# A graph attention whose keys are sorted within and across partitions, with bf16 one-hot sums and the payload in three parts

## The chip, the cores and the metric

The kernel runs on one core of a Trainium2 chip. The metric is the device time of one execution in microseconds (us), taken as the median of several runs. The profile comes from one further execution; its instructions are counted from the first one's start.

## The reference, cut to what matters

Four layers follow each other on 6250 nodes of 256 features, each with a layer norm before it and its result added to x. The change lies in the second: an attention over 131072 random edges (both ends drawn from 0 to 8191, so that many fall outside the nodes), whose result chooses two of four experts for each node.

```python
h = (x_flat @ W_gat).reshape(M, HEADS, NUM_EXPERTS)          # 4 x 4
a_src = (h * att_src).sum(-1); a_dst = (h * att_dst).sum(-1)
e = leaky_relu(a_src[src] + a_dst[dst], negative_slope=0.2)
ee = exp(e - segment_max(e, dst)[dst])
denom = segment_sum(ee, dst, num_segments=M)
msg = h[src] * (ee / (denom[dst] + 1e-16))[:, :, None]
agg = segment_sum(msg, dst, num_segments=M).reshape(M, 16) + b_gat
scores = layernorm(agg).reshape(M, HEADS, NUM_EXPERTS).mean(1)
topk_s, topk_i = top_k(scores, 2); w = softmax(topk_s)
for ei in range(4):                                          # 256 -> 512 -> 256
    out += gate(ei) * (gelu(x @ W1[ei] + b1[ei]) @ W2[ei] + b2[ei])
```

The first layer is a graph layer over 106250 edges with 256 attributes each (sorted by destination), the third a graph layer over the same edges with one weight each, the fourth a small mixture of experts. Source indices beyond the last node count as the last node; edges with a destination outside the nodes are left out.

## The kernel before, in words

The nodes lie in T = 49 blocks of 128. Three stages follow each other.

**Edge stage** (loop over `q` in the function's middle, to about 1555 us). The first layer's edges come in 147 groups (`groups1`, three a block of nodes). Each group is turned on DVE (`turn`, L1487 on), multiplied on PE (`hidden`), joined with gathered rows on DVE (`join`, L1505), rectified on ACT and summed on PE (`add_up`, L1512). [...]the order of the queues is the order of the program text here (`Ordered.pin`). Beside it runs other work, one generator step at a time (`steps`, L1611): `sort` is the sorting of the attention's keys, one step a group, and `slow` the preparation of the edges' windows.

Sorting: each partition holds C2 = 1024 of the attention's edges as integer keys (destination in the high bits, source in the low 13), made by `make_keys`. `sort_steps` (L1284) is a bitonic sort of the 1024 keys within each partition: 55 passes, each of a max and a min (L1299, L1300), the first 45 in two runs. `sorted_edges` (L1307) then takes the keys apart into the source (`src2`), the block of the destination (`high`) and its place in the block (`low`), writes `low` turned to DRAM (`low_dram`), and compares all blocks with limits (L1329 to L1338), so that an edge outside its limits starts `general_path` at the end.

**Attention stage** (loop `for k in range(NA + 5)`, L2208, 1555 to about 2830 us). A tile is one column of the sorted keys: one edge from each of the 128 partitions. A row `g` is eight tiles; there are NA = 80 rows. Since each partition is sorted by itself, a row's edges fall into a band of up to NK = 12 blocks (`near_blocks`, L932; 9.9 blocks in the mean). Row `g` goes through these steps, in iterations g, g+2, g+3, g+4 and g+5 of the loop:

- `fetch` (L1793): eight gathers on POOL of the source nodes' 24 values, five buffers.
- `score` (L1798): rb, the turned `low` broadcast from DRAM, is compared with the partition number (L1806, DVE), and PE multiplies the resulting one-hot rows with `part`, the destination scores of the band in three bf16 parts, into pa (L1810, three matmuls a tile). A (L1818) is the one-hot choice of the block.
- `weigh` (L1824): za = pa times A, reduced over blocks, plus the source's score, leaky, exponential (ACT).
- `spread_out` (L1838), in halves of four tiles: the payload (16 values and 4 denominators times the exponential, L1845, in PSUM as px) is spread over the band, pp = payload times A (L1852), 20 columns a block; B (L1861) is the one-hot place in the block, fp32.
- `add_up` (L1866): for each tile one fp32 matmul of B with pp, 20 columns a block, summed over the eight tiles in po (L1873); then acc += po (L1879, DVE).

Between these stand "slots" (`slot`, L2187): each issues one step of the second layer's experts (`experts1`; four fp32 matmuls ph or py of 256 columns, L1115), in the first 62 iterations five a row and then four, 396 steps in all, and steps of the node work. `count_last` (L1882) counts the edges whose source is the last node, by columns 544 to 848, eight at a time, two groups an iteration. When the sums of a range of blocks are complete (`complete`), `gates` makes the choice of experts and `node_values` the next layer's table `hp_dram`. ys of the experts are loaded back by `load_outputs` into eight buffers.

**Last stage** (from about 2875 us): gathers of `hp_dram` (831 on POOL), the third layer's sums and the fourth layer.

Of the kernel before, what the change touches and what calls it, by code (L numbers as in the profile page):

```python
# [16 lines left out]
P = 128  # L17
# [10 lines left out]
class Ordered:  # L28
# [6 lines left out]
    def pin(self):  # L35
# [16 lines left out]
        self.at = self.traced[-1]  # L52

# [815 lines left out]
def kernel(ctx: ExitStack, tc: tile.TileContext, a: dict, out: bass.AP):  # L869
# [49 lines left out]


    KA, KB, KT, KM, NK = 640, 544, 848, 596.0, 12
# [3 lines left out]
    assert C2 % 8 == 0 and KA % P == 0 and P % G == 0 and N <= 8192 - P and T >= NK  # L925
# [5 lines left out]

    def near_blocks(g):  # L932

        k = g * G + G / 2
        mid = k * (N / KM) / P
        spread_of = (C2 * (k / C2) * (1 - k / C2)) ** 0.5 * (N / KM) / P
        n = min(NK, int(-(-2 * (4.2 * spread_of + 0.9) // 1)))
        b0 = min(max(round(mid - n / 2), 0), T - 2)
        return b0, min(max(round(mid - n / 2) + n, b0 + 2), T) - b0
# [4 lines left out]
    with ExitStack() as fast:  # L944
# [12 lines left out]
        lane16 = const.tile([P, P], BF16, name="lane16")  # L957
        with tc.tile_pool(name="numbers", bufs=1) as numbers:
# [6 lines left out]
            V.tensor_copy(lane16, jn)  # L965
# [281 lines left out]
        src2 = gat.tile([P, KA], I32, name="src2")  # L1247
        low = gat.tile([P, KT], BF16, name="low")
        high = gat.tile([P, KT], BF16, name="high")
        good3 = gat.tile([P, 2, 2], F32, name="good3")  # L1250

        def make_keys(ix, k):
# [4 lines left out]
            for i in range(2):  # L1257
# [22 lines left out]
                raw[1], raw[1], 13, 0x10000000, op0=OP.logical_shift_left, op1=OP.bitwise_or  # L1280
# [3 lines left out]
        def sort_steps():  # L1284


            here, there = key, order
            size = 2
            while size <= C2:
                step = size // 2  # L1290
                while step:
# [13 lines left out]
            assert here is order  # L1305

        def sorted_edges(pst, wk):  # L1307

            k = order.bitcast(I32)[:, 0:KT]
            V.tensor_scalar(src2, k[:, 0:KA], 8191, None, op0=OP.bitwise_and)  # L1310
            some = key[:, 0:KT]
            for v, s in ((high, 20), (low, 13)):
                vi = some.bitcast(I32)
                V.tensor_scalar(
                    vi, k, s, 127, op0=OP.logical_shift_right, op1=OP.bitwise_and
                )
                V.tensor_copy(some, vi)
                V.tensor_scalar(some, some, -1.0, 127.0, op0=OP.mult, op1=OP.add)
                V.tensor_copy(v, some)
            for c in range(KA // P):  # L1320
                pt = pst.tile([P, 4, P], F32, name="pt")
                TE.transpose(pt[:, 0, :], some[:, c * P : (c + 1) * P], ident)
                lt = wk.tile([P, P], BF16, name="lt")
                SC.activation(lt, pt[:, 0, :], AF.Copy)
                SC.dma_start(low_dram[c * P : (c + 1) * P, :], lt)
            V.tensor_add(good2[:, 1:2], good3[:, 0, 0:1], good3[:, 1, 0:1])
            V.tensor_add(good2[:, 3:4], good3[:, 0, 1:2], good3[:, 1, 1:2])

            lim = key[:, 0:KA]  # L1329
            for g in range(KA // G):  # L1330
                V.memset(lim[:, g * G : (g + 1) * G], float(near_blocks(g)[0]))
            hit = order[:, 0:KA]
            V.tensor_tensor(hit, high[:, 0:KA], lim, op=OP.is_ge)
            for g in range(KA // G):
                V.memset(lim[:, g * G : (g + 1) * G], sum(near_blocks(g)) - 0.5)
            V.tensor_tensor(lim, lim, high[:, 0:KA], op=OP.is_ge)
            V.tensor_mul(hit, hit, lim)
            V.tensor_reduce(good2[:, 0:1], hit, axis=AX.X, op=OP.add)  # L1338
# [5 lines left out]
        with ExitStack() as layer:  # L1344
# [113 lines left out]
            HS = D + 8  # L1458
            with (
# [144 lines left out]
                def sorting():  # L1604

                    yield from sort_steps()
                    sorted_edges(psm, wk)
# [13 lines left out]
                for q in range(NQ1 + 2):  # L1621
# [15 lines left out]
                    steps()  # L1637
# [19 lines left out]
        acc = sums.tile([P, T, HV], F32, name="acc")  # L1657
# [101 lines left out]
        with (  # L1759
# [4 lines left out]
            tc.tile_pool(name="pa3", bufs=2, space=PSUM) as psa,  # L1764
            tc.tile_pool(name="po3", bufs=1, space=PSUM) as pso,
            tc.tile_pool(name="px3", bufs=1, space=PSUM) as psx,
# [9 lines left out]
            px = psx.tile([P, P + 2 * G * HV], F32, name="px")  # L1776
            lanes = px[:, 0:P]
            V.tensor_copy(lanes, lane)
# [3 lines left out]
            NA = KA // G  # L1782
# [55 lines left out]
            def spread_out(g, half):  # L1838
# [18 lines left out]
                if half == 1:  # L1857
                    near.pop(g)
# [789 lines left out]
```

## Time and profile before

| | |
|---|---|
| median of 3 runs | 4254.52 us (4244.25 to 4271.54) |
| profiled execution | 4184.73 us |
| its span, first to last instruction | 4182.9 us |
| mean granted TensorE clock | 0.857 |
| busy: PE, PEld, DVE, ACT, POOL | 3303.4, 2578.7, 2138.8, 1127.3, 2249.3 us |
| attention: matmuls po (L1873) | 1280 records, 261.1 us busy |
| attention: matmuls pa (L1810, bf16) | 1920, 76.8 us |
| experts: ph and py (L1115) | 1600 and 1568 records, 417.1 and 408.4 us |
| gathers in the three stages | 882, 640 and 831 on POOL |

PE is TensorE's matmuls, PEld its weight loads, DVE VectorE, ACT ScalarE, POOL GpSimd, SP the engine that issues most transfers. A group's row gives line, engine, operation, output and inputs, shape, count, then busy us and mean ns, then the idle time of the engine just before the group and what ended it ("issue": nothing that the profile shows; "remote": an event that it can't place). An fp32 matmul has two records. Records overlap in the pipeline, so that their mean is longer than their distance, and busy times of groups can overlap too.

### The profile page before, as it was taken

The numbers are of one execution on the slowest core, as the hardware profiler recorded it, in microseconds if no ns is written. First come the engines' busy times: TensorE is split into PE (matmuls) and PEld (weight loads), VectorE is DVE, ScalarE is ACT, GpSimd is POOL, SyncE is SP. The second block draws the span as 40 slices with busy tenths as digits, with TensorE's granted clock in tenths as the row PEclk, the third lists the DMA queues.
The fourth block names the chain that finished last, engine by engine and source line by source line (L and its number), as shares of the span: only waits on it lengthen the run. The fifth ranks groups of instructions, "written<-read, shape, count | busy, mean of one in ns | idle before, by whom it ended". The sixth has DMA issues, their size and how long they took to land.

```text
span 4182.9 us, 57093 instructions
## 1 busy us (share of the span) xinstructions
PE 3303.4 (79%) x18509; PEld 2578.7 (62%) x18509; DVE 2138.8 (51%) x5571; ACT 1127.3 (27%) x2014; POOL 2249.3 (54%) x2364
## 2 busy tenths in 40 slices
PE   6888888898898885888898998786256866767788
PEld 5566666666576664677787777674245544555566
DVE  6566566665554444656455657555223333333344
ACT  4122222222222222333434344452001211111123
POOL 0656556566565634455454545534666666666651
PEclk8899999999899997999999999896557677767778
DMA  5677777777676742323333334333111111111210
GB/s 174 158 176 167 163 168 168 162 169 163 154 176 164 168 109 53 82 66 89 88 81 101 97 85 111 72 77 95 44 47 49 51 50 49 51 49 51 53 50 20
DMA packets 699200, 428.56 MB, mean 102 GB/s; under 512 B 531305, under 2 KB 640348, under 8 KB 698893
## 3 DMA queue, kind: packets, MB, share of 16 engines
q0 software_dynamic: 89408, 178.08, 18.4%
q1 hardware_dynamic: 366236, 187.21, 16.9%
q10 hardware_dynamic: 243248, 59.52, 7.2%
q8 instruction: 150, 2.46, 0.3%
q14 instruction: 158, 1.29, 0.1%
HBM read 382.05 MB, written 42.49 MB: 101 GB/s over the span
## 4 chain that ended last, share of the span: by engine, by line
PE 50%; another core or an unknown queue 18%; DVE 7%; issue 6%; ACT 3%; DMA 1%; POOL 0%; SPq 0%; ACTq 0%; DVEq 0%
PE ph L1115 22%; PE py L1115 10%; PE pe L2513 5%; PE pt L1115 4%; PE po L1873 4%; PE pe L1531 3%; PE pa L1810 1%; DVE eq L2492 1%; PE pt L1109 1%; DMA rb<-low_dram 1%; ACT hh L1709 1%; PE pe L2508 1%; ACT L1709 0%; DVE x_all L2054 0%
## 5 line engine op out<-in xcount | busy, mean ns | idle before, releaser
L1128 POOL DMA_INDIRECT h<-y_dram,src x882 | 846.6, 960 | 666.5 <-issue 508.4
L1128 POOL DMA_INDIRECT hg<-hp_dram,src x831 | 785.7, 946 | 457.8 <-issue 229.1
L1128 POOL DMA_INDIRECT sg<-gat_dram,src x640 | 612.0, 956 | 623.0 <-DVE px L1845 339.0
L1115 PE MATMUL ph<-w1b,et 128*128 128x256 f32 x3528 | 863.3, 397 | 35.9 <-issue 25.7
L1115 PEld LDWEIGHTS ph<-w1b,et 128*128 128x128 f32 x3528 | 677.5, 197 | 205.3 <-issue 115.9
L2513 PE MATMUL pe<-eq,hg 128*128 128x96 f32 (+15 forms) x2036 | 372.6, 331 | 158.3 <-issue 100.6
L2513 PEld LDWEIGHTS pe<-eq,hg 128*128 128x128 f32 x2036 | 359.0, 250 | 224.9 <-issue 157.8
L1508 DVE TENSOR_TENSOR h<-ph,h 128x1536 f32<-128x1536 f32 x147 | 258.2, 1757 | 428.8 <-remote 149.4
L1115 PE MATMUL py<-w,hh 128*128 128x256 f32 x1568 | 408.4, 400 | 64.2 <-ACT hh L1709 33.7
L1115 PE MATMUL ph<-b_all,w 128*128 128x256 f32 (+1 forms) x1600 | 417.1, 400 | 11.3 <-issue 9.8
L2492 DVE TENSOR_SCALAR eq<-px,dst,ew 128x96 f32<-128x96 f32 x831 | 262.3, 372 | 319.3 <-remote 137.4
L1509 ACT ACTIVATE h<-h 128x1536 f32<-128x1536 f32 x147 | 218.2, 1485 | 725.4 <-DMA ea<-in_edge_attr_dram 293.2
L1115 PEld LDWEIGHTS py<-w,hh 128*128 128x128 f32 x1568 | 300.3, 199 | 118.1 <-ACT hh L1709 41.7
L1115 PEld LDWEIGHTS ph<-b_all,w 128*128 128x128 f32 x1600 | 307.8, 202 | 55.4 <-issue 16.6
L1531 PE MATMUL pe<-h,eq 128*32 128x257 f32 x3168 | 257.2, 412 | 41.2 <-issue 40.9
L1873 PE MATMUL po<-pp,B 128*128 128x240 f32 (+10 forms) x1280 | 261.1, 344 | 17.2 <-DVE acc L1879 7.1
L1709 ACT ACTIVATE hh<-ph,b 128x256 f32<-128x256 f32 (+1 forms) x400 | 165.7, 466 | 392.0 <-remote 151.0
L1490 DVE STREAM_TRANSPOSE et<-ea 128x1536 f32<-128x1536 f32 x147 | 260.5, 1773 | 13.1 <-issue 9.5
L1873 PEld LDWEIGHTS po<-pp,B 128*128 128x128 f32 x1280 | 220.4, 194 | 32.0 <-issue 8.4
L1531 PEld LDWEIGHTS pe<-h,eq 128*32 128x32 f32 x3168 | 106.1, 115 | 148.0 <-issue 100.9
L1115 PE MATMUL py<-ew,g 65*128 65x256 f32 x392 | 136.5, 474 | 68.2 <-DVE x_all L2468 58.2
L1852 DVE TENSOR_TENSOR pp<-px,A 128x960 f32<-128x960 f32 (+10 forms) x160 | 156.3, 977 | 39.9 <-remote 27.5
(339 smaller groups left out, 3808.8 us busy)
## 6 DMA issues: line engine op xcount, KB each, us to landing
ea<-in_edge_attr_dram ACTq DMA_DIRECT2D x588, 96.0 KB
ea<-in_edge_attr_dram SPq DMA_DIRECT2D x588, 96.0 KB
y<-y SPq DMA_DIRECT2D x196, 128.0 KB
w<-in_L_ffn_W_dram SPq DMA_DIRECT2D x48, 512.0 KB
y<-ys SPq DMA_DIRECT2D x96, 256.0 KB
rb<-low_dram SPq DMA_DIRECT2D x80, 256.0 KB
h<-y_dram,src POOLq DMA_INDIRECT x882
hg<-hp_dram,src POOLq DMA_INDIRECT x831
```

The lines of the kernel that those rows point to most:

```text
L1109: TE.transpose(pt[:, c, :], src[:, c * P : (c + 1) * P], ident)
L1115: TE.matmul(dst, lhs(c), rhs(c), start=c == 0, stop=c == n - 1)
L1128: GP.indirect_dma_start(out=dst, out_offset=None, in_=table[0:NP, :], in_offset=IndirectOffsetOnAxis(ap=idx, axis=0),)
L1490: V.transpose(et[q].rearrange("p c m k -> p m c k"), ahead.pop(q).rearrange("p i m (c k) -> p (i m) c k", c=2),)
L1508: V.tensor_add(h, ph.pop(q), h)
L1509: SC.activation(h, h, AF.Relu)
L1531: TE.matmul(sums[w][b * Q : (b + 1) * Q, :], eq[k][:, j, at], h[:, i * NT + j, 0:WS], start=g == 0 and j == NT - 1, stop=g == last_of[b] a ...
L1709: SC.activation(hidden[u][:, f, :n, :], ph[:, f - f0, :n, :], AF.Gelu, bias=b1[:, e, f : f + 1],)
L1852: V.tensor_tensor(pps[g, half][:, :, 0:n, :], pay[:, js, :].unsqueeze(2).to_broadcast([P, HG, n, HV]), near[g][:, js, 0:n].unsqueeze(3).to ...
L1873: TE.matmul(po.rearrange("p b v -> p (b v)"), B[:, j, :], pp[:, j, 0:n, :].rearrange("p b v -> p (b v)"), start=half == 0 and j == 0, stop ...
L2492: V.tensor_scalar(equals[k][:, j, :], lanes[:, 0:NW], dst_of[:, t : t + 1], ew[:, t : t + 1], op0=OP.is_equal, op1=OP.mult,)
L2513: TE.matmul(sums[b][:, lo - t0 * P : hi - t0 * P], hg[:, j, :], eq[:, j, lo - n0 : hi - n0], start=False, stop=after >= (t0 + n) * P,)
```

## The change

**Sorting across partitions.** `sort_steps` gets an argument `least` and is run twice. The first run sorts within partitions and stops the last merge at steps of 8, so that each group of eight columns holds the right eight keys, in no order. `turn_keys` turns the keys on PE (eight transposes, two ACT copies), so that partition r holds row r's 1024 keys from all partitions; the second run sorts these, stopping the last merge at steps of 128; a second turning brings them back. A tile then holds 128 keys that follow each other in a whole row. Each step is still a max and a min and a `yield`; `sort` is now advanced twice in odd groups. `sorted_edges` yields between its parts, and its comparison with limits goes.

**Fewer blocks a tile.** `sorted_tiles` works out on the host, for each tile, which blocks its edges can fall into. For these sizes there are NA = 84 rows, 73 of them with eight tiles, 612 tiles together; a tile covers 1 to 7 blocks, 2116 in all, and a row a union of up to 14. `block` holds for each edge its block less the first of its tile; its starting values are written by 379 POOL memsets when the kernel starts.

**Sums.** For each tile E is a one-hot [128, blocks x 128] in bf16: one DVE `tensor_scalar` compares the numbers `nodes16` with the edge's number (`bits`), both as bf16 patterns. The payload is split into three bf16 parts (`weight`), which with a column of ones make 61 columns (`pays`, two buffers). PE multiplies E, a block at a time, with the payload; a row's sums lie in two PSUM banks of up to eight blocks each, the first with two buffers, the second with one. acc has 61 columns a block; `gates` adds the three parts, and the ones count the edges for the check at the end.

```diff
-        def sort_steps():
+        def sort_steps(here, there, least):
...
-                while step:
+                while step >= (least if size == C2 else 1):
...
+        def turn_keys(pst, here, there):
+            for k in range(0, G, 4):
+                pt = pst.tile([P, 4, P], F32, name="pt")
+                for i in range(4):
+                    TE.transpose(pt[:, i, :], here[:, :, k + i], ident)
+                SC.activation(there[:, k : k + 4, :], pt, AF.Copy)
+                yield
+        def sort_all(pst):
+            yield from sort_steps(key, order, G)
+            yield from turn_keys(
+                pst, key.rearrange("p (r k) -> p r k", k=G),
+                order.rearrange("p (k r) -> p k r", k=G),
+            )
+            yield from sort_steps(order, key, P)
+            yield from turn_keys(
+                pst, order.rearrange("p (k r) -> p r k", k=G),
+                key.rearrange("p (r k) -> p k r", k=G),
+            )
...
-                    steps()
+                    steps(*([sort] if q % 2 else []))
...
-                got[g] = wk.tile([P, G, GW], F32, name="sg", bufs=5)
+                got[g] = wk.tile([P, G, GW], F32, name="sg", bufs=4)
...
+            def weight(g, step):
+                m = len(tiles2[g])
+                parts = [pays[g % 2][:, 0:m, i * HV : (i + 1) * HV] for i in range(3)]
+                if step == 0:
+                    pay[g] = wk.tile([P, G, HV], F32, name="pay", bufs=1)[:, 0:m, :]
...
+                    SC.activation(parts[0], pay[g], AF.Copy)
+                elif step == 1:
+                    V.tensor_sub(pay[g], pay[g], parts[0])
+                    SC.activation(parts[1], pay[g], AF.Copy)
+                else:
+                    V.tensor_sub(parts[2], pay.pop(g), parts[1])
+            def spread_out(g, j):
...
+                n = tiles2[g][j][1]
+                Es[g, j] = wk.tile([P, NM, P], BF16, name="E", bufs=EB)
+                V.tensor_scalar(
+                    Es[g, j][:, 0:n, :].rearrange("p b k -> p (b k)"), nodes16[:, 0 : n * P],
+                    bits.bitcast(F32)[:, g * G + j : g * G + j + 1], None, op0=OP.is_equal,
+                )
+            def add_up(g, j):
...
+                    pos[g] = [
+                        pso.tile([P, 512], F32, name=f"po{i}", bufs=2 - i) for i in range(2)
+                    ]
...
+                for b in range(b0, b0 + n):
+                    bank, to = divmod(b - u0, UB)
+                    TE.matmul(
+                        pos[g][bank][:, to * HP : (to + 1) * HP], E[:, b - b0, :],
+                        pays[g % 2][:, j, :], start=bank not in begun,
+                        stop=bank not in later and (b == b0 + n - 1 or to == UB - 1),
+                    )
+                    begun.add(bank)
+                if j == len(tiles2[g]) - 1:
+                    po = pos.pop(g)
+                    for k in range(0, u1 - u0, UB):
...
+                        V.tensor_add(
+                            some, some,
+                            po[k // UB][:, 0 : n * HP].rearrange("p (b v) -> p b v", v=HP),
+                        )
```

The order within an iteration k of the attention's loop, with EB = 6 buffers of E and LAG = 4 tiles between writing and use:

```diff
+                now, here, there = k - 2, k - 3, k - 4
+                def spread_and_sum(i):
+                    for q in (2 * i, 2 * i + 1):
+                        if there in range(NA):
+                            spread_out(there, q)
+                        g, j = divmod(there * G + q - LAG, G)
+                        if g in range(NA):
+                            add_up(g, j)
...
+                    weight(there, 1)
+                spread_and_sum(0)
                 slot()
                 if now in range(NA):
                     score(now, 0)
                 slot()
...
+                    weight(there, 2)
+                spread_and_sum(1)
                 if here in range(NA):
                     weigh(here)
...
                 slot()
+                spread_and_sum(2)
                 slot()
                 if now in range(NA):
                     score(now, 1)
                 run(routing, False)
                 slot(int(k < 62))
+                    weight(here, 0)
+                spread_and_sum(3)
+                for _ in range(4):
                     if last_columns:
+                        count_last(*last_columns.pop(0))
```

**The rest.** `count_last` takes the columns that can hold the last node's edges at most four at a time (65 groups, 215 columns), four groups an iteration. The checks and the last node's values that `last_edges` made are made in `own_edges`, at k = 1. lanes and the payload leave PSUM for SBUF; pa has one tile with two halves. za and A are narrower, by the blocks of a row's widest tile. `load_outputs` puts even blocks' outputs into the table `gtab`, which is free by then, instead of four of the eight buffers.

## The prediction

> **What bounds the kernel now.** First the page's strips of forty slices.
>
> ```profile
> PE   6888888898898885888898998786256866767788
> DVE  6566566665554444656455657555223333333344
> POOL 0656556566565634455454545534666666666651
> ...
> PEclk8899999999899997999999999896557677767778
> ```
>
> There are three stages: edges until about slice 14, attention with the first experts until about 27, then the last graph layer. The table of stretches gives each a number (PE, weight loads, DVE, ACT, POOL; clock; DMA share; GB/s):
>
> ```profile
> 300.00:1050.00 750.00, 655.76 (x4037) 487.87 (x4036) 462.58 (x851) 171.64 (x287) 452.27 (x469) 0.94 0.74 167
> 1200.00:1500.00 300.00, 252.05 (x1580) 189.09 (x1581) 141.34 (x213) 68.28 (x115) 178.00 (x188) 0.91 0.71 164
> 1560.00:2830.00 1270.00, 1062.22 (x6818) 910.41 (x6818) 720.81 (x1765) 501.17 (x873) 611.06 (x639) 0.93 0.34 83
> 2880.00:4100.00 1220.00, 813.29 (x3266) 597.14 (x3266) 429.19 (x1587) 189.70 (x337) 779.84 (x826) 0.70 0.19 49
> ```
>
> In the attention stage PE is busy 1062 of 1270 us (84%), DVE 57%, POOL 48%. PE sets its length. In the last stage PE's clock is down at 0.70 and POOL issues a gather every 1220 us / 826 = 1.48 us; nothing of the change is in it, so it only starts earlier or later.
>
> Which part of PE's work is the attention's sum? The groups of the page, and the timeline of one row in its middle:
>
> ```profile
> L1873 PE MATMUL po<-pp,B 128*128 128x240 f32 (+10 forms) x1280 | 261.1, 344 | 17.2 <-DVE acc L1879 7.1 <-issue 6.5 <-DVE x_all L2054 3.4
> L1852 DVE TENSOR_TENSOR pp<-px,A 128x960 f32<-128x960 f32 (+10 forms) x160 | 156.3, 977 | 39.9 <-remote 27.5 <-PE ph L1115 6.0 <-PE po L1873 3.4
> L1806 DVE TENSOR_SCALAR rb<-rb,pid 128x1024 bf16<-128x1024 bf16 x80 | 39.1, 489 | 50.1 <-DMA rb<-low_dram 47.4 <-issue 2.6
> ```
> ```profile
> 2212.27 1.78 PE L1873 MATMUL po<-pp,B 128*128 128x240 f32 x8
> 2213.89 1.89 PE L1115 MATMUL ph<-b_all,w 128*128 128x256 f32 x8
> 2215.62 0.46 PE L1810 MATMUL pa<-part,rb 128*128 128x48 bf16 x12
> 2215.92 0.46 PE L1115 MATMUL py<-w,hh 128*128 128x256 f32 x1
> ```
>
> Busy times of neighbouring groups overlap, so I price by starts. Half a row of sums (four fp32 matmuls, two records each) takes 2213.89 - 2212.27 = 1.62 us, 405 ns a matmul of 240 columns; a slot of expert work 2215.62 - 2213.89 = 1.73 us; twelve bf16 pairs of load and matmul 0.30 us, 25 ns each. From 2100 to 2550 us 29 rows passed, 15.5 us each, with 14.0 us of busy PE and 1.5 us of waits in each. A row's PE work by starts: 5.1 slots 8.9, sums 3.24, scores 0.6, node values about 0.7.
>
> [...]
>
> **The change part by part.**
>
> *Sorting (edge stage).* Sorting goes from 100 to 190 pairs of max and min (97, then 93), with 16 transposes and four ACT copies between. Pairs cost 2 x 0.43 us: 90 x 0.86 = 77 us more DVE work. They are placed after the turn, in every other group. What hides them: an edge group takes 750 us / 79 turns = 9.5 us while sorting runs beside it (300 to 1050) and 300 / 31 = 9.7 us after it has ended (1200 to 1500), so a pair per group costs nothing now; DVE then is busy 62%, and half a pair more per group (0.43 us) leaves it below 70%. Only turn and join are due within a group, 3.5 of about 9.6 us. Uncovered, it would be 77 us. The steps number about 200 and 1.5 are taken per group: done near group 135 of 147, before attention. The transposes add 16 x 0.3 = 5 us to PE; the burst of memsets and comparisons at 1076 to 1090 us, about 14 us of DVE, goes. I take 0, and -10 to +40 for the range.
>
> *379 small POOL memsets at the start*, about 0.12 us each by the page's start-up memsets, 45 us; POOL is busy 2.5 us before its first gather at 103 us. Hidden; at 0.25 us each it would still be 95.
>
> *PE in attention.* Removed: 640 fp32 matmuls. By 405 ns at 12 blocks, in proportion to the 9.9 blocks of the mean row and a little more for short rows: 225 us (the 261 of the row overlaps). Added: 612 tiles with together 2116 matmuls, 61 columns[...]. At 25 ns for 48 columns[...], I take 30 ns: 63 us. Bounds: 25 ns (53 us) and 50 ns (106 us), if loads don't overlap. PE loses 160 us of work.
>
> *DVE in attention, a row of 8 tiles.* Removed: two pp 2.30, two B 1.36, za 0.56, its reduction 0.84, acc 0.40, A 0.25, px 0.33: 6.0 us. Added: E, by the rb row a fixed 0.22 us plus 0.033 us a block: 8 x 0.22 + 27.9 x 0.033 = 2.7; za on 208 elements 0.39 and reduction 0.56 (the 224 forms); A 0.2; payload and two subtractions 3 x 0.33; acc in two banks, 488 and some 290 elements, 0.66 + 0.46 by the 1.04 ns an element of the other forms: 6.0 us. DVE's row stays at 8.9 us (256 us of 450 in 29 rows).[...]
>
> *Counting the last node's edges.* 65 groups of at most four columns, four a row, instead of 38 of eight, two a row. PE waits for each: 63 us now, of which 34 are the wait for expert weights at the start. Per group: b 0.6, q 0.3, matmuls and their latency 0.4, count 0.2, so 1.5 us a group, 6 a row, against 5. In the first 17 rows, whose sums are short anyway, this eats what PE saves: 0 for these rows.
>
> *New waits.* (1) E has six buffers and is used four tiles later; DVE at tile q waits for PE's tile q-6, and behind it stand ys, rb and A. PE needs E two slots (3.5 us) after DVE may write it, for 0.3 us of work: seldom late. (2) The second and third part of the payload go DVE, ACT, DVE, ACT, DVE; ACT's copy stands behind the last slot's two gelus (0.84 us), DVE's rb comparison stands behind the subtraction, and PE's scores wait for rb. I allow 0.5 us a row. (3) acc's add of two banks holds DVE where it now holds it for one; the first bank has a second buffer, so PE goes on. (4) gathers have four buffers instead of five, freed one row earlier: no change. In all 2.0 us of PE waits a row, against 1.5.
>
> *Rows.* New full row: 8.9 + 0.84 + 0.6 + 0.7 + 2.0 = 13.0 us. Before, from the eighteenth row's score (1894 us) to the last (2820): 926 us. After: 45 rows x 13.0 = 585; 13 rows with four slots and 38 blocks 12.5 = 163; nine short rows (15 tiles in all) 7.5 = 68: 816. Gain 110. Experts end with the rows (398 slots for 396 steps) where now a dozen remain after them, some 10 us of the 55 between the last score and the first gather of the next stage: gain 10. own_edges and gates gain some ten DVE instructions and sixteen small adds: under 5 us, beside the wait for weights.
>
> Sum: -120 us. The profiled execution (4184.7, span 4182.9) would be 4065. The median of the runs is 70 us above it; taking the same 120 from it gives **4135**.
>
> **Rivals.**
>
> *Same, rows paced by something else (chance 0.17).* POOL's eight gathers take 8 x 1.25 = 10 us a row (0.94 busy and 0.30 issue)[...]; with buffers coming late besides, 14.6 us a row costs the 58 long rows 58 x 1.6 = 93 of the 120: 4227. For it: POOL now waits most for px, that is, for buffers, so it has slack of 5 us a row only. Against: gathers now show 956 ns beside rb and 946 in the last stage.
>
> *Slower (0.13): hand-offs tile by tile.* Now PE takes four tiles on one wait, then each of 612. If in-order DVE comes late to each by 0.55 us, 4.4 us a row takes the place of the 2.0: 15.4 us. The 58 long rows then lose 58 x 2.4 = 139, the first 17 some 1.5 each, 25: the gain of 120 becomes a loss of 44: 4300. It decides from 0.5 us a tile (58 x 2.1 = 120). For it: DVE stands at the row's acc until PE's last tile (56 us of waits in 29 rows). Against: between two such points it has 9 us of work for 13.
>
> *Faster still (0.20): no new waits,* 1.5 us a row, PE pairs at 25 ns, counting hidden: 12.3 us a row, the first 17 also 1 us shorter: 120 + 58 x 0.7 + 17 = 178: 4077.
>
> *It doesn't do what it says (under 0.01):* an edge outside its tile would start the general path after everything, and the time would be a multiple.
>
> **Chances and range.** Forecast 0.50, faster still 0.20, same 0.17, slower 0.13. About 1% (42 us) is what a measurement can tell from no change. The first two lie below 4212; so faster 0.70, same 0.17, slower 0.13. The forecast's own range: E and pairs at their bounds (+43 us of PE), sorting -10 to +40, waits of 1.5 to 2.7 us a row (-29, +40): 4080 to 4205. Reaching to both sides for eight in ten: 4060 to 4260.
>
> **What would show it.** Right: po group near 2116 records with under 110 us busy; E about 0.33 us mean; rows of 13 us between 1950 and 2550; edge groups still 9.5 to 9.7 us; the first gather of hp near 2755 instead of 2876. Wrong: edge groups above 10 us (sorting not hidden); PE idle before po on DVE E (hand-offs); gathers above 1.1 us or POOL without waits for buffers[...]; scores waiting on rb or ACT (the chain of parts).

## The result and the profile after

The comparison on record gives the kernel after a median of 4270.74 us (4252.54 to 4293.68, 20 runs) against 4252.93 us (4232.87 to 4271.54, 20 runs) for the kernel before: ratio 1.0045, 95% interval 1.0028 to 1.0062, so 0.45% slower, little but clear of the noise. Forecast was 4135, in a range of 4060 to 4260. The profiled execution of after took 4285.28 us with a span of 4283.5 us; that of before, at 4184.73, lay 68 us under its own median and 48 under the fastest of its 20 runs, so the pair of profiles shows a difference of 100 us where the medians have 18.

This number depends on the occasion on which it was taken, and without that the rest can't be understood. Six later groups of runs, on four chips (9, 11, 4 and 15 on record), put the same kernel before at 3434 to 3436 us each time; the unchanged kernel after took 3356 us in one of them, on chip 9 (ratio 0.9768, 0.9744 to 0.9792). The chip of the comparison on record isn't noted in its results, so the record can't tell whether the chip or the moment made the difference. "First comparison" and "later runs" below mean these two.

The strips of the page after, in the first comparison:

```profile
PE   6798888888888785777887877785346777877787
...
DVE  7576666666555444545463544575123333333344
...
POOL 1655655566565544345454444422666666665651
PEclk9899999999999897888998988796567667677678
```

The attention stage now runs to slice 27 or 28, and PE's digits in it are mostly 7 and 8 under a granted clock of mostly 8 and 9 tenths, where before had mostly 8s and 9s under 9s. The table of stretches (PE, weight loads, DVE, ACT, POOL; clock; DMA share; GB/s); the attention stage starts and ends later than in before, and its stretch is moved with it:

```profile
300.00:1050.00 750.00, 644.20 (x3956) 481.17 (x3951) 478.01 (x908) 168.97 (x285) 451.38 (x463) 0.93 0.73 164
1200.00:1500.00 300.00, 245.22 (x1490) 179.61 (x1488) 156.85 (x260) 67.02 (x115) 170.03 (x175) 0.90 0.69 155
1590.00:2960.00 1370.00, 1025.80 (x7622) 822.64 (x7622) 727.93 (x2538) 582.20 (x1109) 594.90 (x612) 0.86 0.32 83
2970.00:4190.00 1220.00, 840.76 (x3254) 626.98 (x3254) 423.24 (x1571) 190.15 (x337) 772.75 (x820) 0.68 0.18 49
```

PE's busy share of the attention stretch fell from 84% to 75%, and its clock from 0.93 to 0.86: PE has less to do and does it slower. From the page's groups, the new instructions:

```profile
L1964 DVE TENSOR_SCALAR E<-nodes,bits 128x256 bf16<-128x256 bf16 (+5 forms) x612 | 187.6, 340 | 194.4 <-remote 73.3
L1986 PE MATMUL po<-pays,E 128*128 128x61 bf16 x2116 | 120.0, 199 | 48.1 <-issue 41.8
```

The counts are as forecast and E is (340 ns against 0.33 us). But PE was idle 41.8 us ahead of po on "issue", which means that the profile shows nothing it waited for. In before, "issue" ahead of po was 6.5 us. The list of waits of the same stretch (waiting group, releaser, us in total, times, longest) has more of the kind, on ScalarE and VectorE too, "remote" being an event that the profile can't place:

```profile
ACT hh L1787 <- remote: 166.5, 26, 29.7
DVE E L1964 <- remote: 73.3, 29, 8.0
PE py L1160 <- issue: 55.7, 57, 3.7
PE po L1986 <- issue: 41.8, 54, 2.5
```

The timeline of such a place shows it best (start, us, engine, line, operation; in brackets the idle time before and its end):

```profile
2446.17 0.19 PE L1986 MATMUL po<-pays,E 128*128 128x61 bf16 x1 [0.54 <-issue]
2446.87 0.11 PEld L1986 LDWEIGHTS <-E 128*128 128x128 bf16 x2 [1.32 <-issue]
2446.89 0.19 PE L1986 MATMUL po<-pays,E 128*128 128x61 bf16 x1 [0.53 <-issue]
2447.60 0.19 PE L1986 MATMUL po<-pays,E 128*128 128x61 bf16 x1 [0.52 <-issue]
2447.60 0.10 PEld L1986 LDWEIGHTS <-E 128*128 128x128 bf16 x1 [0.62 <-issue]
2448.30 0.25 PE L1986 MATMUL po<-pays,E 128*128 128x61 bf16 x3 [0.51 <-issue]
...
2448.57 0.84 ACT L1787 ACTIVATE hh<-ph,b 128x256 f32<-128x256 f32 x2 [5.33 <-PE po L1986]
```

Pairs of weight load and matmul on the same bank, which elsewhere follow each other every 30 ns, start one at a time every 0.71 us. By the program, nothing that they need was outstanding: E is written four tiles ahead, the payload once a row, and the bank already takes sums. Below, a record that starts 0.65 to 0.76 us behind the one before it is called late. In the attention stage of the first comparison 43 of 13,913 PE records (matmuls and weight loads) were late before and 123 of 15,267 after; in the edge stage 78 and 72.

What ended PE's waits in 44 full rows of that stage (18 to 62, counted from the step of `weigh` that makes z leaky) can be listed too; these are lines of the two lists (us in total, times, longest), first before, then after:

```profile
PE py L1115 <- ACT hh L1709: 24.9, 12, 4.1
PE py L1115 <- issue: 8.7, 7, 2.3
```

```profile
PE py L1160 <- issue: 38.0, 41, 3.7
PE py L1160 <- ACT hh L1787: 31.7, 15, 4.8
PE po L1986 <- issue: 30.1, 42, 1.9
PE py L1160 <- ACT pays L1954: 4.0, 3, 2.7
```

Over all lines, waits on "issue" grew from 19 to 89 us in these rows, waits for ScalarE from 47 to 57. No wait for E stands in the list of after.

Later runs have next to no late records: 4 to 6 in the same stage. The same table there, first the kernel before, then after:

```profile
300.00:1050.00 750.00, 731.02 (x4831) 565.21 (x4830) 545.60 (x1128) 208.20 (x352) 538.81 (x563) 0.99 0.97 200
1300.00:2340.00 1040.00, 1013.52 (x6970) 897.18 (x6968) 756.81 (x1890) 525.70 (x931) 616.19 (x643) 0.99 0.44 108
2350.00:3380.00 1030.00, 875.16 (x3402) 642.13 (x3402) 442.05 (x1640) 200.54 (x356) 778.60 (x826) 0.72 0.23 59
```

```profile
300.00:1050.00 750.00, 732.95 (x4822) 568.37 (x4820) 572.09 (x1075) 207.13 (x346) 542.00 (x563) 0.99 0.96 200
1320.00:2265.00 945.00, 881.65 (x7639) 747.39 (x7637) 724.78 (x2554) 581.25 (x1111) 610.25 (x615) 0.97 0.48 121
2275.00:3300.00 1025.00, 871.69 (x3381) 640.30 (x3381) 437.80 (x1631) 197.82 (x353) 774.81 (x822) 0.72 0.23 59
```

Here PE is busy 97% of the attention stage before and 93% after, at 0.99 and 0.97 of its clock, and the stage is 95 us shorter. By stages, from the starts in the four traces (later: b_again2 and a_again):

| us | first: before | first: after | later: before | later: after |
|---|---|---|---|---|
| edge stage, first to last turn | 1408.8 | 1437.0 | 1154.2 | 1170.3 |
| attention, first gather of sg to first of hg | 1316.6 | 1376.8 | 1042.1 | 946.6 |
| a gather of the last stage | 1.478 | 1.487 | 1.249 | 1.248 |
| a full row (18 to 62) | 15.44 | 16.17 | 13.16 | 11.27 |
| of it, starts of matmuls up to 0.6 us apart | 13.42 | 11.98 | 12.93 | 10.90 |
| of it, gaps over 0.6 us between starts | 2.02 | 4.18 | 0.23 | 0.36 |
| half clock in these 44 rows | 55 | 154 | 0 | 7 |

Longer packets are not the difference: a packet of the plain transfers took 26.4 ns in the mean in the first trace of before and 27.5 in the later one, of the gathers 138 and 147 ns.

The page of before carried a sign of the difference that the prediction did not use. This is its chain of work that ended last, by what it consists of, and below it the same chain of the same kernel later (b_again2). The kernel runs on one core, so the second term names nothing in it:

```profile
PE 50%; another core or an unknown queue 18%; DVE 7%; issue 6%; ACT 3%; DMA 1%; POOL 0%; SPq 0%; ACTq 0%; DVEq 0%
```

```profile
PE 63%; POOL 13%; issue 8%; DMA 7%; DVE 5%; ACT 2%; SPq 1%; ACTq 0%; DVEq 0%; POOLq 0%
```

### The profile page after: what moved, and what is told of

Same layout as the page of the kernel before. It is cut to its first block, busy times and chain, and to the rows that moved or that the text cites. A ratio compares the mean times of both kernels' runs of the same rounds, so it can differ in the third digit from the quotient of the medians.

```text
span 4283.5 us, 59672 instructions
## 1 busy us (share of the span) xinstructions
PE 3272.3 (76%) x19189; PEld 2500.2 (58%) x19189; DVE 2166.2 (51%) x6247; ACT 1188.7 (28%) x2203; POOL 2257.1 (53%) x2720
## 4 chain that ended last, share of the span: by engine, by line
PE 36%; another core or an unknown queue 14%; issue 6%; DVE 5%; ACT 3%; DMA 1%; POOL 1%; DVEq 0%; ACTq 0%; SPq 0%
PE ph L1160 13%; PE py L1160 11%; PE pe L2662 5%; PE pt L1160 2%; PE po L1986 2%; PE pa L1909 1%; DVE eq L2641 1%; POOL hg L1173 1%; DVE E L1964 1%; DVE x_all L2617 1%; ACT L1787 0%; ACT hh L1787 0%; PE pe L1609 0%; PE pt L1154 0%
## 5 line engine op out<-in xcount | busy, mean ns | idle before, releaser
L1173 POOL DMA_INDIRECT h<-y_dram,src x882 | 858.4, 973 | 669.0 <-issue 485.7
L1173 POOL DMA_INDIRECT sg<-gat_dram,src x612 | 593.8, 970 | 723.1 <-DVE pay L1946 313.8
L1160 PE MATMUL ph<-w1b,et 128*128 128x256 f32 x3528 | 868.2, 398 | 32.8 <-issue 26.9
L1160 PEld LDWEIGHTS ph<-w1b,et 128*128 128x128 f32 x3528 | 680.3, 198 | 204.4 <-issue 114.3
L1160 PE MATMUL py<-w,hh 128*128 128x256 f32 x1568 | 454.0, 428 | 105.6 <-issue 54.5
L2662 PEld LDWEIGHTS pe<-eq,hg 128*128 128x128 f32 x2036 | 375.3, 261 | 189.8 <-issue 117.5
L2662 PE MATMUL pe<-eq,hg 128*128 128x96 f32 (+15 forms) x2036 | 386.4, 342 | 126.2 <-issue 67.2
L1160 PE MATMUL ph<-b_all,w 128*128 128x256 f32 (+1 forms) x1600 | 458.9, 426 | 11.8 <-issue 11.5
L1160 PEld LDWEIGHTS py<-w,hh 128*128 128x128 f32 x1568 | 308.1, 210 | 171.1 <-issue 70.2
L1160 PEld LDWEIGHTS ph<-b_all,w 128*128 128x128 f32 x1600 | 316.9, 214 | 55.5 <-issue 17.4
L1964 DVE TENSOR_SCALAR E<-nodes,bits 128x256 bf16<-128x256 bf16 (+5 forms) x612 | 187.6, 340 | 194.4 <-remote 73.3
L1160 PE MATMUL py<-ew,g 65*128 65x256 f32 x392 | 146.6, 503 | 57.5 <-DVE x_all L2617 42.1
L1986 PE MATMUL po<-pays,E 128*128 128x61 bf16 x2116 | 120.0, 199 | 48.1 <-issue 41.8
L1160 PE MATMUL ph<-b_all,ew 128*128 128x512 f32 (+2 forms) x256 | 115.4, 576 | 53.4 <-ACT g L2577 33.8
```

Of the source, the lines that this page charges most:

```text
L1160: TE.matmul(dst, lhs(c), rhs(c), start=c == 0, stop=c == n - 1)
L1173: GP.indirect_dma_start(out=dst, out_offset=None, in_=table[0:NP, :], in_offset=IndirectOffsetOnAxis(ap=idx, axis=0),)
L1964: V.tensor_scalar(Es[g, j][:, 0:n, :].rearrange("p b k -> p (b k)"), nodes16[:, 0 : n * P], bits.bitcast(F32)[:, g * G + j : g * G + j + 1 ...
L1986: TE.matmul(pos[g][bank][:, to * HP : (to + 1) * HP], E[:, b - b0, :], pays[g % 2][:, j, :], start=bank not in begun, stop=bank not in lat ...
L2662: TE.matmul(sums[b][:, lo - t0 * P : hi - t0 * P], hg[:, j, :], eq[:, j, lo - n0 : hi - n0], start=False, stop=after >= (t0 + n) * P,)
```

## The experiments

Times are medians; "before" beside each is the kernel before, run on the same chip together with it (3434 to 3436 us throughout). Variants of the kernel after are compared with its 3356.42 us, which was measured once, on chip 9; the held kernels ran on chips 11, 4 and 15.

**b_again, b_again2: before unchanged.** No edit.

> The kernel before, unchanged, for a profile beside the others of this call: the profiled execution of before (4185 us) lies about 70 us under the median of its runs (4253), so its gaps and its clock may flatter it. Both theories need its row: dense work of PE, gaps over 0.6 us between matmul starts, time at half clock. If the good profile was typical of the kernel, the span is near 4185 and the attention stage again 1317 us from first gather to first gather of the next stage; if it was a lucky one, the span is near 4250 and some 60 us more of gaps and half clock stand in the attention stage.

> The kernel before, unchanged, for a profile beside the kernel after on this chip. On a chip like that of the second call: span near 3434 us, edge groups of 7.9 us, a gather of the last stage every 1.25 us, row 12.5 us. On a chip like the first: 4180 to 4270, 9.6, 1.48 and 15.3.

3436.16 and 3431.45 us: neither number that the first expectation offered. Everything is shorter than in the first comparison, the edge stage by 18% and a gather of the last stage by 15%, in the same program. So the first comparison had something over its kernels that belongs to neither. PE's late records alone are too few for it: 78 of them can't make the 255 us of the edge stage.

**a_again: after unchanged.**

> The kernel after, unchanged. In the call before this one the kernel before took 3435 us, not 4253: no gap of 0.70 us between PE's records, 14 us of gaps over 0.6 us in rows 18 to 74 (138 in the first comparison), 6 us at half clock (82). Theory of the held engines: on the chip of the first comparison every engine's next instruction came late in places, and this ate the gain; on a chip like that of the second call the change is faster by 80 to 120 us (ratio 0.965 to 0.977), rows take about 11 us, gaps over 0.6 us stay under 40 us. Theory of the change's own waits: the hand-offs cost on any chip, the ratio stays 1.00 to 1.01, and gaps of 50 us or more stand beside po and py. If this call falls on a chip like the first, times are near 4250 and 4270 and the gaps as in the first two profiles.

3356.42 us (3350.14 to 3361.39), ratio 0.9768 (0.9744 to 0.9792), gaps 16 us in 44 rows. Just at the near end of what the theory of the held engines asked for (80 to 120 us; 79 measured); gaps of every kind are 0.36 us a row, and the theory that the change's own waits cost on any chip is out.

**b_sort2: 100 more pairs of the sort.**

```diff
                     steps()
+                    if sort:
+                        pair_again()
```

`pair_again` issues the last max and min once more from the same source.

> The kernel before, with the last pair of max and min of the sort issued a second time in every edge group, after the turn, where the change puts its extra pairs: 100 more pairs (86 us of VectorE), same values. If a pair beside an edge group is hidden, as the prediction has it, the groups of 300 to 1050 us stay at 9.5 us and the time at that of before (0 to +10 us). If the extra sorting is what made the edge stage 27 us longer after the change (about 90 pairs), these 100 pairs cost 25 to 35 us. If nothing hides them, 86 us.

3436.69 us, ratio 1.0004 (0.9996 to 1.0013): hidden, below 5 us for 100 pairs. In the later runs the extra pairs are not what lengthened the edge stage; in the first comparison, where groups took 9.6 us in place of 8.0, this kernel was not run.

**b_scores2: 1920 more short pairs in before.**

```diff
-                for j in range(half * HG, (half + 1) * HG):
+                for j in [*range(half * HG, (half + 1) * HG)] * 2:
```

> The kernel before, with the 24 short bf16 pairs (weight load and matmul) of each row's scores issued twice: 1920 short pairs more, about as many as the 2116 of the change, without any new wait on another engine, same values. Theory of the short pairs (they themselves starve PE or drop its clock): 100 us or more slower, with new stretches in which PE starts one record every 0.7 us. Theory of the hand-offs (the waits between VectorE, ScalarE and PE cost, not the pairs): 1920 x 25 ns = 48 us at most, and no such new stretches.

3480.88 us, ratio 1.0141 (1.0121 to 1.0161): 46 us, 24 ns a pair, and no late records to speak of. In this run short pairs cost their pitch and nothing more. The theory of the short pairs is out for the later runs; about the first comparison, where records come late, this run can't speak.

**a_merged: some 700 instead of 2116 pairs.**

```diff
+                    c = min(UB - to, b0 + n - b)
                     TE.matmul(
-                        pos[g][bank][:, to * HP : (to + 1) * HP], E[:, b - b0, :],
-                        pays[g % 2][:, j, :], start=bank not in begun,
...
+                        pos[g][bank][:, to * HP : (to + c) * HP], some,
+                        flat[:, 0 : c * HP], start=True, stop=True,
...
```

The payload's columns are the weights here and E streams, so the kernel leaves out the right sums.

> The kernel after, with the matmuls of a tile that go to one bank put together into one of c x 61 columns: same columns streamed, same E, payload, banks and waits, but some 700 instead of 2116 pairs (the sums come out wrong: the product is not the reference's, and the sign to start the general path is left out). Theory of the short pairs: the gaps go with them, 60 to 110 us less than the kernel after, so 4160 to 4210. Theory of the hand-offs: it gains the 25 ns of some 1400 weight loads at most, 35 us, and keeps the gaps: 4235 to 4270.

3329.97 us, ratio 0.9705 (0.9683 to 0.9726), 26 us less than after, with 736 matmuls in place of 2116. That is the hand-offs' column (at most 35 us), where gaps were small to begin with; about the gaps of the first comparison this run says nothing. Nor is it a price of 19 ns a pair: by the traces the sums themselves, from start to start, take 56 us in place of 63. Matmuls of 61, 122, 183 and 427 columns start 28, 53, 79 and 181 ns apart, so that each further 61 columns cost 25 to 26 ns and a pair of its own only 3 or so on top. Where the other 20 us come from is open; the edge stage, which the edit leaves alone, was 11 us shorter in this trace.

**b_held, a_held, b_heldV, a_heldV: VectorE and ScalarE late.**

```diff
                 slot()
+                hold(k)
```

`hold` issues ten products of 128x128 on VectorE and, in the first two kernels, 21 copies on ScalarE in every third row. By the traces it took 232 us of VectorE and 175 of ScalarE; the lumps were drawn out to 6 and 11 us, other work in between.

> The kernel before, with ScalarE and VectorE made late in the attention stage on purpose, about as the first comparison's traces show them late without a cause: in each of 80 rows ten idle products on VectorE (about 3 us), in every third row 21 idle copies on ScalarE (about 6 us), behind the scores of the first half. Same values. Theory that the change has less slack: before hides most of it, 30 to 100 us slower than before. Rival, that both kernels pay alike: whatever before pays, the kernel after pays too.

> The kernel after with the same idle work in the same places. Theory that the change has less slack (VectorE feeds PE tile by tile half a row ahead, ScalarE stands twice between VectorE and the payload, PE has less work of its own to cover them): it pays 60 us or more beyond what before pays, and the advantage of 79 us (ratio 0.977 of the two without idle work) is gone or nearly. Rival: both pay alike and it stays about 80 us ahead; then the loss on the chip of the first comparison came from PE's own instructions being late.

> The kernel before with the idle work on VectorE alone (about 3 us in each of 80 rows), to part the two engines. Theory of less slack: under 60 us. Both alike: whatever it is, the next kernel pays the same.

> The kernel after with the idle work on VectorE alone. Theory of less slack: 30 us or more beyond what before pays for the same. Both alike: within 15 us of it.

Before pays 30 us for both (3464.62) and 15 for VectorE alone (3450.04); after pays 18 (3374.30) and 19 (3375.52). The theory that the change has less slack falls for lateness of this kind: it pays no more than before, and stays 75 to 90 us ahead.

**a_count7: counting in groups of seven, two a row.**

```diff
-                for _ in range(4):
+                for _ in range(2):
```

with groups of 7 for HG = 4 in `last_columns` and in the tiles b and q.

> The kernel after, with the last node's edges counted in groups of up to seven columns, two a row, instead of four columns, four a row (same values). The prediction gave 65 groups at 1.5 us as what eats the gain of the first 17 rows. If so, half as many groups give back 0.75 us for each group saved, some 20 to 25 us off 3356. If PE is short of no time there on a chip like that of the second call (rows 3 to 17 take 10.8 us, as the later ones do), nothing: within 8 us. On a chip like the first, times near 4270 minus the same.

3352.74 us, ratio 0.9747 (0.9718 to 0.9776): 4 us, no more than one kernel's runs differ by. Counting eats next to nothing.

**a_onebank: one buffer for the first bank.**

```diff
-                        pso.tile([P, 512], F32, name=f"po{i}", bufs=2 - i) for i in range(2)
+                        pso.tile([P, 512], F32, name=f"po{i}", bufs=1) for i in range(2)
```

> The kernel after, with one buffer for the first bank of a row's sums as well (this part of the change undone, same values). PE then can't begin the next row's sums before VectorE has added the bank to acc. The prediction has PE go on because of the second buffer. If it carries weight, PE waits about one addition and VectorE's place in its queue, 0.7 to 2 us in each of 73 full rows: 50 to 150 us slower than 3356. If slack covers it, since four tiles lie between: under 15 us.

3360.62 us, ratio 0.9769 (0.9744 to 0.9796): 4 us. The second buffer carries next to nothing here; slack covers the addition.

**b_heldPE, a_heldPE: tiny products between PE's other work.** In every third row eight tiny products on PE, each waiting for ScalarE's copy of the one before.

> The kernel before with PE itself held: in every third of 80 rows eight tiny products on PE, each of which waits for ScalarE's copy of the one before it, so that PE starts a record only every 0.5 to 0.8 us for 4 to 6 us, as the first comparison's traces show it without a cause (27 such stretches; same values). PE sets the end here, so most of it is paid: 100 to 170 us.

> The kernel after with the same stretches. Theory A, that one stretch costs the kernel after more (PE's clock falls further afterwards, or the hand-offs to VectorE spread it): 50 us or more beyond what the kernel before pays, which would explain the loss of the first comparison by the same number of stretches. Theory B, that a stretch costs both alike and the kernel after only met more of them there (123 late records against 43 in its attention stage): within 25 us of what before pays, and the advantage of about 80 us stays.

27 and 22 us (3462.25, 3378.90), where 100 to 170 were expected of before. Inconclusive: the traces show 14 to 96 other matmuls between the eight, so PE was not held.

**b_pinPE, a_pinPE: PE held for certain.** Ten products in 25 rows, with the order of PE's instructions kept around them.

```diff
+                for _ in range(10):
+                    TE.matmul(pt, idle, idle[:, 0:32], start=True, stop=True)
+                    SC.activation(idle[:, 0:32], pt, AF.Copy)
```

> The kernel before with PE held for certain: ten tiny products, each waiting for ScalarE's copy of the one before, and now no other PE instruction may be ordered between them (in the two runs before this one PE's other work slipped in, so that nothing was held). 25 rows, each held 10 x 0.55 = 5.5 us, 137 us in all; same values. Expected: 100 to 150 us slower than before, and the clock falls to half for some windows behind the stretches.

> The kernel after with the same 25 pinned stretches. Theory A (one stretch costs the kernel after more): 50 us or more beyond what the kernel before pays. Theory B (a stretch costs both alike; on the chip of the first comparison the kernel after met more of them): within 25 us of what before pays, about 3460 to 3500.

3630.83 us (ratio 1.0572, 1.0542 to 1.0603) and 3586.83 us (1.0438, 1.0407 to 1.0468): 197 us on before, 230 on after. The expectations missed: 100 to 150 us for before, and for after either 50 us beyond before (A) or within 25 of it (B); it is about 33. A stretch in the timeline of a_pinPE, and the table of stretches for the attention stage of b_pinPE and then a_pinPE:

```profile
1931.75 0.19 PE L2354 MATMUL py<-idle 128*128 128x32 bf16 x1 [0.35 <-ACT idle L2355]
1932.29 0.19 PE L2354 MATMUL py<-idle 128*128 128x32 bf16 x1 [0.35 <-ACT idle L2355]
1932.83 0.19 PE L2354 MATMUL py<-idle 128*128 128x32 bf16 x1 [0.35 <-ACT idle L2355]
```

```profile
1300.00:2530.00 1230.00, 1110.71 (x7193) 956.11 (x7193) 754.57 (x1882) 580.65 (x1180) 615.88 (x642) 0.93 0.37 91
```

```profile
1320.00:2490.00 1170.00, 973.76 (x7879) 805.32 (x7878) 734.60 (x2555) 627.49 (x1356) 600.91 (x615) 0.89 0.39 97
```

The first record of a stretch to the last makes 140.5 us in before and 175.8 in after, where each copy waits in line with more work of ScalarE (627 us busy against 581). The attention stage grew by 196.1 and by 228.2 us: 1.40 and 1.30 us for each us that PE was held. Per us, both pay about alike, as theory B has it; the 33 us more on after go with stretches that are 35 us longer.

What is paid above 1, 56 and 52 us, can be read from the clock. It fell from 0.99 to 0.93 and from 0.97 to 0.89, with 179 and 250 us of the stage at half (17 and 62 without the stretches). Of these, 45 and 85 us lie within the stretches, so outside them half-clock time grew by 117 and 103 us. In the attention stage of the first trace of after, records of the experts' matmuls (L1160, 128x256) start 216 ns apart at the full clock and 427 at half (medians). If work here took twice as long at half clock too, the added time costs half of itself, an estimate of 58 and 51 us: just the surplus. Half clock begins between the start of a stretch and 7 us behind its end in 25 and 24 of the 25 stretches. The kept order without the products was not run, so a share of its own isn't excluded.

In the first trace of after, the half-clock pieces around 2350 to 2490 us last 3.41 or 6.83 us each. In the two pinned kernels the clock fell while PE went on starting a tiny matmul about every 0.54 us.

## Why the prediction was wrong

**The step that failed** is the paragraph "New waits", and in it the sentence "In all 2.0 us of PE waits a row, against 1.5." In the first comparison the gaps in a full row went from 2.0 to 4.2 us. None of the waits that the paragraph names made them: PE waited for no E in these rows and 4 us in all for the payload's parts (0.1 a row, where 0.5 was allowed), gaps of every kind come to 0.36 us a row in the later runs, and idle work on VectorE and ScalarE hurt after no more than before. Of the growth, 70 us in 44 rows or 1.6 a row, is "issue": PE's own instructions starting late while it waited for nothing shown. The waits for ScalarE (1.3 us a row after) were nearly as long before (1.1).

What failed is that the prediction carried the 1.5 us over as the kernel's own and as fixed. In the later runs that row has 0.2, and the signs stood on the page of before: "issue" waits, and 18% of the chain under an unknown queue. The profile of before was an unusually quick execution, so 2.2 us a row is what this pair of traces has; between typical runs the growth may be less.

**How the loss adds up.** By the medians, the first comparison takes 818 us more than the later runs before the change (4253 - 3435) and 914 after it (4271 - 3356): 96 us more, which is the gain of 79 and the 18 on top (each rounded). The profiles show where such time lies, not its exact size, since lateness differs from execution to execution: they have 753 and 924 us. 156 of these 171 us more are in the attention stage (274 before, 1316.6 - 1042.1; 430 after, 1376.8 - 946.6). In the 44 full rows the gaps cost 2.02 - 0.23 = 1.8 us a row more than in the later runs before, and 4.18 - 0.36 = 3.8 after; dense work 0.5 and 1.1 more, with 55 and 154 us at half clock. So a row's gain of 1.9 us met 2.6 us of additional loss, which is the 0.7 us by which rows got longer (15.44 to 16.17).

The two pinned kernels show that held PE time is paid 1.3 to 1.4 times by either kernel, which speaks for a difference in the amount of lateness and not in its price. That the pinned stretches cost what the lateness of the first comparison did is argued, not shown. Why after met more of it stays open. It did not pick the short pairs: 64 of the 123 late records after were bf16, as were 55% of all its records in that stage, and 13 of 43 before, of 32%. No run shows more, since the lateness came back in none of the later runs; b_scores2 and a_merged would have to be run where it does. What makes the engines late is open as well.

**Sums of PE.** Right: "30 ns: 63 us", where the step from 25 ns at 48 columns, which the trace of before shows, to 30 at 61 was the author's estimate. In the later trace of after the 2116 pairs take 63 us from start to start once gaps are taken out, and b_scores2 gives 24 ns for its narrower ones. The timeline there, with bursts between slots:

```profile
1901.80 0.46 PE L1986 MATMUL po<-pays,E 128*128 128x61 bf16 x10
1902.10 1.97 PE L1160 MATMUL ph<-b_all,w 128*128 128x256 f32 x8
1903.91 0.45 PE L1909 MATMUL pa<-part,rb 128*128 128x28 bf16 x12
```

Ten pairs take 1902.10 - 1901.80 = 0.30 us. The sign "under 110 us busy" for this group came out as 120.0 in the first comparison and 101.9 in the later trace.

**Rows.** "13.0 us" against 15.5 was a slip. The old row from the same terms is 8.9 + 3.24 + 0.6 + 0.7 + 1.5 = 14.9, not 15.5, so my own terms gave a gain of 1.9 us, and 0.6 us in each of 58 rows, 35 of the 120, came from comparing a sum with a measurement. The later runs measure 13.16 - 11.27 = 1.89, which is luck in part: the terms have 2.4 us less work a row and 0.5 more waits, the later traces 2.0 less and 0.1 more. A smaller slip is that the bounds of the range, taken together, reach 123 us above the forecast, where the range has 70.

**Sorting.** "0, and -10 to +40": right for the pairs (b_sort2). The edge stage grew by 28 us in the first and 16 in the later traces; in the later one groups 129, 134 and 135, where the sort's end is worked, take 14.7, 12.2 and 14.8 us, as group 100 of before took 20.0. Groups 125 to 139 together are 15 us longer than in before, groups 95 to 104 10 us shorter and the first 60 7 us longer, which is 12 of the 16; why the first 60 are longer is left open. The 379 memsets were hidden: the first gather came at 103 to 105 us, 1 to 3 us later than in before.

**DVE.** Right: E 345 ns in the later trace, payload and subtractions 303 to 308, za 331 and its reduction 460. "A fixed 0.22 us plus 0.033 us a block" was the author's estimate, since one row of 489 ns can't give both numbers. The first trace of after bears it out: E takes 253 ns in the mean for one block, 293 for two, 327 for three and 461 for seven, so about 35 ns for each further block. **POOL.** The rival of rows paced by POOL's gathers did not come: a gather of sg took 990 ns in the later trace of after against 956 in the first of before.

**Counting, banks.** "0 for these rows" was right in effect, for another reason: the first 18 rows gained 9 us in the later runs, and a_count7 shows that groups cost about nothing. The second buffer of the first bank, which the prediction has keep PE going, is worth about 4 us, if anything.

**The rivals.** The outcome of the first comparison, 18 us slower, is nearest to "same", but not by its mechanism, since gathers did not pace the rows: POOL waited 314 us for the payload there; "slower: hand-offs tile by tile" is refuted (0.36 us of gaps a row in the later runs where it asked for 4.4, and no wait for E in the rows above).

## What to carry to other kernels

Rebuild the old row from the same terms as the new one before you subtract; a sum set against a measurement hands the unexplained rest to the change. A wait on "issue" or "remote" on the path is put down to no line of the kernel (here "issue" went from 19 to 89 us in 44 rows): take another profile of the kernel before, on another occasion, to see whether it stays, and widen the range by what those waits hold, because work that is removed may be given back there. And a gain of 2% found on one occasion may be nothing on another: name the measured pace of an untouched stage (here a gather of 1.25 or 1.48 us) beside every ratio.

## What was not expected of the hardware

One kernel took 4253 and 3435 us, with nearly equal packet times (26.4 and 27.5 ns) and with starts late in steps of about 0.70 us. Of PE's record starts, 164 in the first trace of before lay 0.68 to 0.73 us behind the last, in the later one of b_again 5. On SyncE the same count is 273 and 21, on ScalarE 95 and 48; on VectorE (43 and 41) and GpSimd (9 and 17) it does not show. Its cause is not known.

A PE that starts only a tiny matmul every 0.54 us for about 5 us or more lost its full clock in 49 of 50 stretches, and with that 1.3 to 1.4 us for each us held. By contrast, some 405 us of idle work on VectorE and ScalarE cost 30 us in before and 18 in after.
